# The second layers of a block's MLPs as seven products for eight, with sums made by adding DMAs

## The chip, the cores and the metric

The kernel runs on one core of a Trainium2 chip. The metric is the device time of one execution in microseconds (us); several executions are timed and their median is given. The core's engines each run an instruction stream of their own in program order: PE (TensorE, matrix products), DVE (VectorE), ACT (ScalarE), POOL (GpSimd) and SP (SyncE, which here only issues DMAs). The streams meet at semaphores. DMAs are issued from SP's queue and from POOL's queue. PE accumulates into banks of 128 x 512 numbers.

## The reference

One block of a model with gated cross-attention, on x of 2 x 512 tokens with 1024 numbers each, cut to what matters:

```python
x = x + tanh(g_xattn) * (fake_quant(layernorm(x)) @ fake_quant(ctx))
xt = layernorm(x).reshape(1024, 1024)
gate = ...                        # router: 16 experts in 4 groups, two experts a token
def step(y, p):
    w1, b1, w2, b2, w3, b3, ge = p
    h = silu(xt @ w1 + b1) * (xt @ w2 + b2)          # w1, w2: 1024 x 256
    return y + ge[:, None] * (h @ w3 + b3)           # w3: 256 x 1024
y = scan of step over the 16 experts
z = (silu(xt @ sw1 + sb1) * (xt @ sw2 + sb2)) @ sw3 + sb3      # sw1, sw2: 1024 x 512
x = x + tanh(g_ffn) * (y + z)
```

With these inputs the tokens use two experts in all. The hidden layer then has 512 numbers of the shared MLP and 256 of each expert, 1024 together, and the second layers are one product: h (1024 tokens x 1024) by w3 (1024 x 1024).

## The kernel before

The work has four stages. In the first (to about 100 us) x is normalised and quantised, multiplied with ctx, and the result added to x; x is stored to DRAM as `x_after`, 8 tiles of 128 tokens x 1024 (`xd`, L326). A second layernorm gives the operand of the MLPs. In the second stage the first layers of the shared MLP's first chunks of 128 hidden numbers and the router run.

From here on every product in fp32 is made of three: each operand is split into a high half, made by ACT (a cast, L333), and a low half, made by DVE (a difference, L334), and PE adds high·high, high·low and low·high.

The third stage makes the first layers of the hidden chunks 3 (`s3`) and 4 to 7 (`b4` to `b7`, the experts' chunks), each by a call of `pair` (L400). A pair takes w1's and w2's columns of one chunk and both batch rows as a 2 x 2 block product by Strassen's scheme: seven products of 12 matmuls of 512 columns (`product`, L405, matmul L410), in the order A11·B11, S2·T2, A12·B21, S3·T3, S1·T1, A22·T4, S4·B22, into three banks A, B and C in the order A B A B C B C. The sums S of the inputs are made once, by adding DMAs from POOL's queue (`add_x`, L786). The sums T of the weights are made by `prep_pair` (L378) for the next chunk while a pair runs: DVE makes four sums (L386 to L389) in two new slabs, then the splits. `prep_pair` is a generator: `begin` runs it to its first `yield`, each `go` on to the next, and the lists given to `pair` as `between` say after which product which steps are issued. Between the products a pair's own work on ACT, DVE and POOL makes the gated hidden numbers: ACT copies the first product (L430) and applies silu (L436, L447), DVE adds products (L433 s6, L440 and L443 s7, L446, L452 and the final multiplications L424), POOL multiplies by the router's gates (L421). `done` (L423) stores each half of a chunk to DRAM as `h_all`, from POOL's queue. The step of `between` that is issued after a product stands ahead of that product's own reading instruction on ACT and DVE.

Ahead of pair s3, SP issues the loads of b4's weights (`load_block`, L808, with the loads of L347: `e0a0r`, `e0b0r`) and stores the two experts' gate columns to DRAM as rows (`g_row`, L818), element by element, to be read back as `gates`, broadcast over partitions (L814). Then follow the next chunk's weights (`e0a1r`, `e0b1r`).

The fourth stage, the second layers, is `down_mm` (L871): 8 chunks x 8 tiles of 128 tokens x 2 halves of 512 columns x 3 = 384 matmuls of 512 columns (the last tile's second half in two of 256). `load_down` and `split_down` load the chunks of h and w3 again as 128 x 1024 and split them, the first six of them inside pair b7. Three token tiles are worked chunk by chunk, the others one after the other. `down_load` loads a tile of `x_after` into Y, `down_bias` (L912) adds the shared and the two experts' biases on DVE, scaled by tanh(g_ffn) and, for the experts, the token's gate (24 operations of 128 x 1024), and `down_end` (L916, L917) adds the scaled product and stores the result.

Tiles come from rings: `slab` (17 buffers of 128 x 1024), `octo` (14 of twice that), `temp` (7 of 128 x 512), `bank` (6) and `tbank` (2). A new tile waits until the last use of the buffer it is given has ended.

Of the kernel before, what the change touches and what calls it, by code (L numbers as in the profile page):

```python
# [9 lines left out]
F32 = mybir.dt.float32  # L10
# [8 lines left out]
P = 128  # L19
# [60 lines left out]
def flamingo_block(  # L80
# [19 lines left out]
    def slab(name, dtype, shape=(P, D)):  # L100
        return slabs.tile(list(shape), dtype, tag="slab", name=name)
# [20 lines left out]

    X = [None] * NT
    x_after = [spill.tile([P, D], F32, name=f"x_after{t}") for t in range(NT)]
    h_all = [spill.tile([P, B * S], F32, name=f"h_all{c}") for c in range(NC)]


    dq = [nc.sync]
# [170 lines left out]
    def fn(t, h):  # L299
        nm, r = md_[t]  # L300
        nc.vector.tensor_scalar(xn_[t][:, half(h)], X[t][:, half(h)], nm, r, ALU.add, ALU.mult)  # L301
# [30 lines left out]
    def split(raw, hi, lo):  # L332
        nc.scalar.copy(hi, raw)  # L333
        nc.vector.tensor_tensor(lo, raw, hi.bitcast(F32), ALU.subtract)  # L334
        return hi, lo

    def split_in_one(name, raw):

        both = octo(name, F32R, (P, 2, *raw.shape[1:]))
        return split(raw, both[:, 0], both[:, 1])  # L340
# [37 lines left out]
    def prep_pair(name, wa, wb, W):  # L378


        lo, hi = slice(0, KH), slice(KH, KD)
        two = lambda n: tuple(slab(f"{name}{n}{m}", F32R, (P, KD, P)) for m in "hl")
        ah, al = two("a")
        W["B11"], W["B21"] = (ah[:, lo], al[:, lo]), (ah[:, hi], al[:, hi])
        t13, t24 = slab(f"{name}t13", F32, (P, KD, P)), slab(f"{name}t24", F32, (P, KD, P))
        nc.vector.tensor_tensor(t13[:, lo], wa[:, lo], wb[:, lo], ALU.subtract)  # L386
        nc.vector.scalar_tensor_tensor(t24[:, lo], t13[:, lo], -1.0, wb[:, hi], ALU.mult, ALU.subtract)
        nc.vector.tensor_tensor(t13[:, hi], wb[:, hi], wb[:, lo], ALU.subtract)
        nc.vector.tensor_tensor(t24[:, hi], wa[:, hi], t24[:, lo], ALU.add)  # L389
        split(wa, ah, al)  # L390
        yield
        b22 = slab(f"{name}b22", F32R, (P, KD, P))
        W["B22"] = split(wb[:, hi], b22[:, lo], b22[:, hi])
        yield
        for n, t in (("24", t24), ("13", t13)):
            h, l = split(t, *two(f"t{n}"))
            W[f"T{n[0]}"], W[f"T{n[1]}"] = (h[:, lo], l[:, lo]), (h[:, hi], l[:, hi])
            yield

    def pair(name, W, b1, b2, ci, gates=None, between=()):  # L400


        pa, pb, pc = (bank(f"{name}{n}") for n in "ABC")
# [17 lines left out]
                nc.gpsimd.tensor_tensor(silu, silu, gates[:, ts(b, S)], ALU.mult)  # L421

        def done(h, silu, b):  # L423
            nc.vector.tensor_tensor(h, h, silu, ALU.mult)  # L424
            nc.gpsimd.dma_start(h_all[ci][:, ts(b, S)], h)

        s1, s6, s7, s11 = (temp(f"{name}{n}") for n in ("s1", "s6", "s7", "s11"))
        product(pa, "A11", "B11", True)
# [80 lines left out]
    def sup_post(c, b, got, lo=0, n=S):  # L509
        h = up_post(f"sa{c}_{b}_{lo}", got, sb1c(c), sb2c(c), n)  # L510
        nc.sync.dma_start(h_all[c][:, b * S + lo : b * S + lo + n], h)
# [245 lines left out]
    def go():  # L757
        next(prep[0], None)
# [2 lines left out]
    begin(3, raw3)  # L761
    go()
    go()
    sup_post(0, 1, got, 0, 256)
    go()
    lT = []
# [49 lines left out]
    load_block(SC)  # L816
    for j in range(2):
        nc.sync.dma_start(g_row[j].rearrange("(t p) -> p t", p=P), chosen[j][1])  # L818
    f = lambda fn, *a: (lambda: fn(*a))
    pair("s3", W[3], sb1c(3), sb2c(3), 3, None, (  # L820
        [f(split_x, "S1", s1)],
        [f(split_x, "S4", s4)],
        [f(lambda: begin(SC, raws_up[SC]))],
        [go],
        [go],
        [go, f(load_block, SC + 1), f(load_gates, 0)],
    ))
    down_prep = []
    for n in range(SC, NC):
        j, c = divmod(n - SC, EC)  # L830
        bv = chosen[j][2]
        if n + 1 < NC:
            between = (
                [f(begin, n + 1, raws_up[n + 1])], [], [go], [go], [go], [],
                [f(load_block, n + 2)] if n + 2 < NC else [],
            )
        else:
            between = down_prep
        if c == 0 and j == 1:
            load_gates(1)  # L840
        if n == NC - 1:
            break
        pair(f"b{n}", W[n], bv[:, 0, c : c + 1], bv[:, 1, c : c + 1], n, gates[j], between)


    def expert_row(w, e, c=None):
        if c is None:
            return w[ds(e, 1), :].rearrange("o d -> (o d)").partition_broadcast(P)
        return w[ds(e, 1), ts(c, P), :].rearrange("o p d -> (o p) d")

    def w3_rows(c):
        if c < SC:
            return sw3[ts(c, P), :]
        j, c = divmod(c - SC, EC)
        return expert_row(ew3, chosen[j][0], c)

    hid, w3, raw_down = [], [], {}

    def load_down(c):
        raw_down[c] = slab(f"h{c}r", F32), slab(f"d{c}r", F32)  # L860
        for raw, src in zip(raw_down[c], (h_all[c], w3_rows(c))):
            nc.sync.dma_start(raw, src)

    def split_down(c):
        for n, raw, got in zip("hd", raw_down[c], (hid, w3)):
            if c == 0:
                got.append(split(raw, *(slab(f"{n}{c}{m}", F32R) for m in "hl")))
            else:
                got.append(split_in_one(f"{n}{c}", raw))

    def down_mm(po, t, c, cols):  # L871
        (hh, hl), (wh, wl) = hid[c], w3[c]
        for p, cl in zip(po, cols):
            nc.tensor.matmul(p, hh[:, ts(t, P)], wh[:, cl], start=c == 0, stop=False)  # L874
            nc.tensor.matmul(p, hh[:, ts(t, P)], wl[:, cl], start=False, stop=False)  # L875
        for p, cl in zip(po, cols):
            nc.tensor.matmul(p, hl[:, ts(t, P)], wh[:, cl], start=False, stop=c == NC - 1)  # L877

    def bias_row(name, row):
        bb = slab(name, F32)  # L880
        dq[0].dma_start(bb, row)
        return bb

    n, bv = NC - 1, chosen[1][2]
    load_down(0)
    pair(f"b{n}", W[n], bv[:, 0, 1:2], bv[:, 1, 1:2], n, gates[1], (
        [f(load_down, 1)],
        [f(split_down, 0), f(load_down, 2)],
        [f(split_down, 1)],
        [f(split_down, 2), f(load_down, 3)],  # L890
        [f(split_down, 3), f(load_down, 4)],
        [f(split_down, 4), f(load_down, 5)],
        [f(load_down, 6)],
    ))

    gt = rt("gt", (P, 2, NT))
    for j in range(2):
        nc.vector.tensor_scalar(gt[:, j], chosen[j][1], tgf, None, ALU.mult)
    rows = []

    def load_rows():
        rows.append((bias_row("sb", sb3.partition_broadcast(P)), lambda t: tgf))
        for j in range(2):
            rows.append((bias_row(f"eb{j}", expert_row(eb3, chosen[j][0])), lambda t, j=j: gt[:, j, t : t + 1]))

    def down_load(t):
        X[t] = slab(f"Y{t}", F32)
        nc.sync.dma_start(X[t], x_after[t])

    def down_bias(t):  # L910
        for bb, scale in rows:
            nc.vector.scalar_tensor_tensor(X[t], bb, scale(t), X[t], ALU.mult, ALU.add)  # L912

    def down_end(po, t, cols):
        for p, cl in zip(po, cols):
            nc.vector.scalar_tensor_tensor(X[t][:, cl], p, tgf, X[t][:, cl], ALU.mult, ALU.add)  # L916
            nc.sync.dma_start(of[ts(t, P), cl], X[t][:, cl])  # L917

    halves = [half(0), half(1)]
    first, rest, last = (4, 5, 6), (7, 0, 1, 2), 3  # L920
    po = {t: [bank(f"po{t}_{h}") for h in range(2)] for t in first}
    for c in range(NC):
        if c == 0:
            split_down(5)
        if c == 1:
            load_down(7)
            split_down(6)
        if c == 2:
            split_down(7)
            load_rows()  # L930
            for t in first:
                down_load(t)
        if c == 4:
            for t in first:
                down_bias(t)
        for t in first:
            down_mm(po[t], t, c, halves)
    for t in first:
        down_end(po[t], t, halves)
    order = (*rest, last)  # L940
    for t in order[:2]:
        down_load(t)
    for n, t in enumerate(rest):
        down_bias(t)
        po = [bank(f"po{t}_{h}") for h in range(2)]
        for c in range(NC):
            down_mm(po, t, c, halves)
        down_end(po, t, halves)
        if n + 2 < len(order):
            down_load(order[n + 2])  # L950
    down_bias(last)
    for cl in (slice(0, 512), slice(512, 768), slice(768, 1024)):
        po = [bank(f"po{last}_{cl.start}")[:, : cl.stop - cl.start]]
        for c in range(NC):
            down_mm(po, last, c, [cl])
        down_end(po, last, [cl])
    manual.close()


# [47 lines left out]
                xl(t, h)  # L1007

    def mlp(name, n, up, down, b1, b2, row, scale):
        bb = bias_row(f"{name}bias", row)  # L1010
        for t in range(NT):
            nc.vector.scalar_tensor_tensor(X[t], bb, scale(t), X[t], ALU.mult, ALU.add)
        for c in range(n):
# [97 lines left out]
```

## Time and profile before

| | |
|---|---|
| median of 3 runs | 322.64 us (322.34 to 323.62) |
| profiled execution, its own time | 323.01 us |
| span of that execution in the trace | 321.3 us |
| granted PE clock, mean | 0.994 |
| busy: PE, DVE, ACT, POOL | 95%, 68%, 36%, 28% |
| pair s3, pairs b4 to b7 | 132.4 to 227.5 us |
| second layers on PE | 228.2 to 316.3 us |

The span is what the profiler recorded of one execution; its own time is 1.7 us longer and includes what lies around the span. "Busy" counts an engine's own instructions and not the waiting, nor the issuing of DMAs. A line of the chain of waits has a start, a duration and what it was; a line of a timeline has a start, a duration, the engine, the source line, the operation, and the tile written and those read, with shape and count. A name with "S", "l" or "h" at its end is a sum, a low or a high half. SPq is SP's queue of DMAs, q1 in the list of queues; q0 is POOL's.

### The profile page before, as it was taken

The numbers are of one execution on the slowest core, as the hardware profiler recorded it, in microseconds if no ns is written. First come the engines' busy times: TensorE is split into PE (matmuls) and PEld (weight loads), VectorE is DVE, ScalarE is ACT, GpSimd is POOL, SyncE is SP. The second block draws the span as 40 slices with busy tenths as digits, with TensorE's granted clock in tenths as the row PEclk, the third lists the DMA queues.
The fourth block names the chain that finished last, engine by engine and source line by source line (L and its number), as shares of the span: only waits on it lengthen the run. The fifth ranks groups of instructions, "written<-read, shape, count | busy, mean of one in ns | idle before, by whom it ended". The sixth has DMA issues, their size and how long they took to land.

```text
span 321.3 us, 4424 instructions
## 1 busy us (share of the span) xinstructions
PE 306.1 (95%) x1626; PEld 244.9 (76%) x1631; DVE 218.8 (68%) x360; ACT 116.2 (36%) x176; POOL 88.7 (28%) x130
## 2 busy tenths in 40 slices
PE   8588799999999999999999999999999999999993
PEld 2244695869995988888888888887788888888883
DVE  3869999997476886396657546479762975663261
ACT  2666669676545307361323324057610000000000
POOL 2695678896900322000013131112200000000000
PEclk9799999999999999999999999999999999999999
DMA  6999992029210999246341604459569053332121
GB/s 207 421 380 358 418 313 111 2 81 343 68 34 18 179 184 208 77 94 149 115 128 66 192 36 149 147 196 337 208 210 356 5 195 131 132 131 74 59 98 41
DMA packets 35105, 53.44 MB, mean 166 GB/s; under 512 B 5436, under 2 KB 23172, under 8 KB 35076
## 3 DMA queue, kind: packets, MB, share of 16 engines
q1 hardware_dynamic: 33124, 46.27, 42.0%
q0 software_dynamic: 1952, 6.82, 8.7%
q8 instruction: 15, 0.25, 0.3%
q14 instruction: 14, 0.11, 0.1%
HBM read 36.29 MB, written 12.59 MB: 152 GB/s over the span
## 4 chain that ended last, share of the span: by engine, by line
PE 83%; DVE 4%; DMA 4%; POOL 4%; issue 2%; ACT 2%; SPq 0%; DVEq 0%; POOLq 0%
PE sp L549 11%; PE sp L360 10%; PE po L877 9%; PE po L874 9%; PE po L875 9%; PE at L251 5%; PE b4B L410 3%; PE b6B L410 3%; PE b5B L410 3%; PE s3B L410 3%; DMA h4r<-h_all 2%; DMA X<-in_dram 2%; PE px L306 2%; PE b7A L410 2%; PE b5C L410 2%
## 5 line engine op out<-in xcount | busy, mean ns | idle before, releaser
L875 PE MATMUL po<-d,h 128*128 128x512 f32 (+1 forms) x119 | 44.9, 377 | 0.0
L874 PE MATMUL po<-d,h 128*128 128x512 f32 (+1 forms) x119 | 44.9, 377 | 0.0
L877 PE MATMUL po<-d,h 128*128 128x512 f32 (+1 forms) x119 | 36.9, 377 | 0.0
L251 PE MATMUL at<-cq,qT 128*128 128x512 bf16 x123 | 29.7, 379 | 2.9 <-POOL cq L170 1.7
L916 DVE SCALAR_TENSOR_TENSOR Y<-po,tg,Y 128x512 f32<-128x512 f32 (+1 forms) x17 | 11.4, 715 | 21.4 <-PE po L877 21.3
L875 PEld LDWEIGHTS po<-d,h 128*128 128x128 f32 x119 | 22.4, 188 | 4.1
L874 PEld LDWEIGHTS po<-d,h 128*128 128x128 f32 x119 | 22.4, 188 | 4.1
L877 PEld LDWEIGHTS po<-d,h 128*128 128x128 f32 x119 | 22.4, 188 | 4.1
L251 PEld LDWEIGHTS <-qT 128*128 128x128 bf16 x128 | 12.1, 97 | 15.7 <-issue 3.0
L912 DVE SCALAR_TENSOR_TENSOR Y<-eb,gt,Y 128x1024 f32<-128x1024 f32 x16 | 20.6, 1285 | 0.6
L912 DVE SCALAR_TENSOR_TENSOR Y<-sb,tg,Y 128x1024 f32<-128x1024 f32 x8 | 10.2, 1278 | 10.3 <-DMA Y<-x_after 10.3
L786 POOL DMA_DIRECT2D xf<-xf x8 | 7.2, 931 | 28.8 <-PE plt L649 15.0
L549 PE MATMUL sp<-XH,sb 128*128 128x256 f32 x96 | 14.1, 292 | 0.0
L549 PE MATMUL sp<-XH,sa 128*128 128x256 f32 x96 | 13.7, 288 | 0.0
L316 DVE TENSOR_TENSOR XL<-px,XH 128x512 fp32r<-128x512 f32 x16 | 10.4, 678 | 3.7 <-ACT xf L323 3.7
L549 PEld LDWEIGHTS sp<-XH,sb 128*128 128x128 f32 x96 | 12.3, 191 | 0.5 <-DVE sb L164 0.2
L360 PE MATMUL sp<-XH,sa 128*128 128x256 f32 (+1 forms) x64 | 12.5, 338 | 0.0
L360 PE MATMUL sp<-XH,sb 128*128 128x256 f32 (+1 forms) x64 | 12.5, 338 | 0.0
L549 PEld LDWEIGHTS sp<-XH,sa 128*128 128x128 f32 x96 | 12.3, 192 | 0.1
L272 ACT ACTIVATE xn<-X,s 128x512 f32<-128x512 f32 x16 | 11.4, 716 | 2.1 <-DVE X L263 1.8
L301 DVE TENSOR_SCALAR xn<-X,nm,d 128x512 f32<-128x512 f32 x16 | 11.2, 726 | 1.4 <-POOL d L297 1.3
L183 DVE BATCH_NORM_STATS2 st<-X 128x6 f32<-128x512 f32 x16 | 10.3, 680 | 2.3 <-DMA X<-in_dram 2.3
(499 smaller groups left out, 690.6 us busy)
## 6 DMA issues: line engine op xcount, KB each, us to landing
cr<-in_dram SPq DMA_DIRECT2D x15, 512.0 KB, 9.9
x_after<-X SPq DMA_DIRECT2D x8, 512.0 KB, 4.3
xf<-xf POOLq DMA_DIRECT2D x8, 512.0 KB, 5.1
Y<-x_after SPq DMA_DIRECT2D x8, 512.0 KB, 5.3
out_dram<-Y SPq DMA_DIRECT2D x15, 256.0 KB, 2.0
X<-in_dram SPq DMA_DIRECT2D x7, 512.0 KB, 9.0
h_all<-sa SPq DMA_DIRECT2D x8, 128.0 KB, 1.8
gates<-g_row SPq DMA_DIRECT2D x2, 512.0 KB, 5.3
```

Of the source, the lines that this page charges most:

```text
L251: nc.tensor.matmul(acc[t][h], qT[b][:, t % TB, k, :], cq[b][k // KH][:, k % KH, half(h)], start=(k == 0), stop=(k == KD - 1))
L272: nc.scalar.activation(xn_[t][:, half(h)], X[t][:, half(h)], AF.Square, bias=s[:, h : h + 1], scale=-float(H), accum_out=q[:, h : h + 1],)
L301: nc.vector.tensor_scalar(xn_[t][:, half(h)], X[t][:, half(h)], nm, r, ALU.add, ALU.mult)
L316: nc.vector.tensor_tensor(XL[b][q][p], px_[t, q], XH[b][q][p].bitcast(F32), ALU.subtract)
L360: nc.tensor.matmul(p, wx[:, k, :], xx[b][k // KH][:, k % KH, cols], start=first and k == 0, stop=last and k == KD - 1,)
L410: nc.tensor.matmul(p, w[:, k, :], x[:, k, :], start=f and k == 0, stop=l and k == KH - 1, skip_group_check=not first,)
L549: nc.tensor.matmul(up_[c, lo, i], w[:, k, :], x[0][k // KH][:, k % KH, lo : lo + 256], start=p == 0 and k == 0, stop=p == 2 and k == KD - 1,)
L874: nc.tensor.matmul(p, hh[:, ts(t, P)], wh[:, cl], start=c == 0, stop=False)
L875: nc.tensor.matmul(p, hh[:, ts(t, P)], wl[:, cl], start=False, stop=False)
L877: nc.tensor.matmul(p, hl[:, ts(t, P)], wh[:, cl], start=False, stop=c == NC - 1)
L912: nc.vector.scalar_tensor_tensor(X[t], bb, scale(t), X[t], ALU.mult, ALU.add)
L916: nc.vector.scalar_tensor_tensor(X[t][:, cl], p, tgf, X[t][:, cl], ALU.mult, ALU.add)
```

## The change

Second layers. The second product is made by Strassen's scheme over halves of the tokens (A1, A2), of the hidden numbers (shared, routed) and of the output columns. Seven products, each of 4 token tiles x 4 hidden chunks x 3 matmuls of 512 columns, 48 in all, make 336. Their order is A11·B11, A12·B21, S2·T2, nS3·nT3, A22·T4, S1·T1, S4·B22. The hidden numbers lie in two DRAM tensors (`h_dram`), shared and routed. The sums S of h are made by adding DMAs from DRAM onto a scaled copy or a loaded part (`add_part`), 8 of 512 KB; the sums T of w3 by DVE in place (`less`). The first product belongs to three further quarters of the output: `tell` scales it on ACT and adds it to `x_after` in DRAM by 12 adding DMAs of 256 KB. The other products' results are added to loaded parts of `x_after` by DVE, as before.

Biases. They are added to `x_after` in DRAM: the shared bias row is loaded broadcast (`load_shared_row`, behind the `g_row` stores on SP), multiplied by tanh(g_ffn) on ACT (`shared_row`), and added to the 8 tiles by adding DMAs of 512 KB from POOL's queue (`add_rows`) during pairs s3 and b4; the experts' rows are scaled by the tokens' gates and summed by ACT and DVE into small tiles (`sum_rows`, 16) and added by 16 DMAs of 256 KB (`add_sum`) during b4 to b7.

Weights' sums. `prep_pair` makes them in place, in the raw weights, in another order and with one more `yield`; it needs two slabs fewer. `done` stores h from SP's queue.

The diff, cut to its core:

```diff
-    h_all = [spill.tile([P, B * S], F32, name=f"h_all{c}") for c in range(NC)]
+    h_dram = [spill.tile([P, KH, B * S], F32, name=f"h{n}") for n in ("shared", "routed")]
+    h_all = [h_dram[c // SC][:, c % SC] for c in range(NC)]
...
     def prep_pair(name, wa, wb, W):
-        ah, al = two("a")
-        W["B11"], W["B21"] = (ah[:, lo], al[:, lo]), (ah[:, hi], al[:, hi])
-        t13, t24 = slab(f"{name}t13", F32, (P, KD, P)), slab(f"{name}t24", F32, (P, KD, P))
-        nc.vector.tensor_tensor(t13[:, lo], wa[:, lo], wb[:, lo], ALU.subtract)
-        nc.vector.scalar_tensor_tensor(t24[:, lo], t13[:, lo], -1.0, wb[:, hi], ALU.mult, ALU.subtract)
-        nc.vector.tensor_tensor(t13[:, hi], wb[:, hi], wb[:, lo], ALU.subtract)
-        nc.vector.tensor_tensor(t24[:, hi], wa[:, hi], t24[:, lo], ALU.add)
-        split(wa, ah, al)
+        h, l = split_in_two(f"{name}a", wa)
+        W["B11"], W["B21"] = (h[:, lo], l[:, lo]), (h[:, hi], l[:, hi])
+        nc.vector.tensor_tensor(wa[:, lo], wa[:, lo], wb[:, lo], ALU.subtract)
+        yield
+        nc.vector.tensor_tensor(wb[:, lo], wb[:, hi], wb[:, lo], ALU.subtract)
         yield
         b22 = slab(f"{name}b22", F32R, (P, KD, P))
         W["B22"] = split(wb[:, hi], b22[:, lo], b22[:, hi])
+        nc.vector.scalar_tensor_tensor(wb[:, hi], wa[:, lo], -1.0, wb[:, hi], ALU.mult, ALU.subtract)
+        nc.vector.tensor_tensor(wa[:, hi], wa[:, hi], wb[:, hi], ALU.add)
         yield
-        for n, t in (("24", t24), ("13", t13)):
-            h, l = split(t, *two(f"t{n}"))
+        for n, t in (("32", wb), ("14", wa)):
+            h, l = split_in_two(f"{name}t{n}", t)
...
         def done(h, silu, b):
-            nc.vector.tensor_tensor(h, h, silu, ALU.mult)
-            nc.gpsimd.dma_start(h_all[ci][:, ts(b, S)], h)
+            got = keep[0] if keep and b == 0 else h
+            nc.vector.tensor_tensor(got, h, silu, ALU.mult)
+            nc.sync.dma_start(h_all[ci][:, ts(b, S)], got)
...
+    def load_shared_row():
+        rows["s"] = slab("rows", F32)
+        nc.sync.dma_start(rows["s"], sb3.partition_broadcast(P))
+    def shared_row():
+        nc.scalar.mul(rows["s"], rows["s"], tgf)
+    def load_rows(h):
+        rows[h] = slab(f"row{h}", F32, (P, 2, H))
+        for j in range(2):
+            nc.sync.dma_start(rows[h][:, j], expert_row(eb3, chosen[j][0])[:, half(h)])
+    def sum_rows(h, t):
+        u = sums[h, t] = temp(f"u{h}_{t}")
+        nc.scalar.mul(u, rows[h][:, 0], gt[:, 0, t : t + 1])
+        nc.vector.scalar_tensor_tensor(u, rows[h][:, 1], gt[:, 1, t : t + 1], u, ALU.mult, ALU.add)
+    def add_rows(lo, hi):
+        for t in range(lo, hi):
+            nc.gpsimd.dma_start(x_after[t], rows["s"], accum_op=ALU.add)
+    def add_sum(h, t):
+        nc.gpsimd.dma_start(x_after[t][:, half(h)], sums[h, t], accum_op=ALU.add)
     pair("s3", W[3], sb1c(3), sb2c(3), 3, None, (
-        [f(split_x, "S1", s1)],
-        [f(split_x, "S4", s4)],
-        [f(lambda: begin(SC, raws_up[SC]))],
-        [go],
-        [go],
+        [f(split_x, "S1", s1), load_shared_row],
+        [f(split_x, "S4", s4), shared_row, f(add_rows, 0, 2)],
+        [f(lambda: begin(SC, raws_up[SC])), f(add_rows, 2, 4)],
+        [go, f(add_rows, 4, 6)],
+        [go, f(add_rows, 6, 7)],
         [go, f(load_block, SC + 1), f(load_gates, 0)],
+        [go, f(load_rows, 0)],
     ))
...
+    summed = [7 * n + k for n in range(3) for k in (1, 3, 4, 5, 6)] + [21]
+    for n, k in enumerate(summed):
+        steps[k].append(f(sum_rows, *divmod(n, NT)))
+        steps[k + 1].append(f(add_sum, *divmod(n, NT)))
+    steps[2].insert(0, f(add_rows, 7, 8))
...
+    def tell(t):
+        s = temp(f"u{t}")
+        nc.scalar.mul(s, pa[t], tgf)
+        for to, h in ((t, 1), (TB + t, 0), (TB + t, 1)):
+            nc.gpsimd.dma_start(x_after[to][:, half(h)], s, accum_op=ALU.add)
+    def product(p, a, b, first, post, meanwhile):
+        for t, steps in zip(range(TB), meanwhile):
+            down_mm(p[t], t, a, b, first)
+            post(t)
+            for step in steps:
+                step()
+    high("A12", parts=two)
+    low("A12", parts=two)
+    scaled("S2", "nS3", 1.0)
+    add_part("S2", h_part, 1, 1)
+    for t in range(TB):
+        down_load(t, 0)
+    pa = [bank(f"pa{t}") for t in range(TB)]
+    product(pa, "A11", "B11", True, tell, (
+        [f(low, "B21", parts=two), f(less, "T1", "B12", "B11", "B11")],
+        [f(less, "nT3", "B12", "B22", "B12")],
+        [f(less, "T2", "B22", "T1", "B22"), f(high, "T2", parts=one)],
+        [f(low, "T2", parts=one), f(high, "T2", parts=two), f(low, "T2", parts=two)],
+    ))
...
+    product(pa, "A12", "B21", False, lambda t: down_add(pa[t], t, 0, True), (
+        [f(high, "S2"), f(low, "S2", parts=one)],
+        [f(low, "S2", parts=two), f(scaled, "S4", "S2", -1.0), f(add_part, "S4", h_part, 1, 0)],
+        [f(high, "nS3"), f(low, "nS3", in_slabs, one)], [f(low, "nS3", in_slabs, two)],
+    ))
...
+    product(pb, "A22", "T4", False, lambda t: down_add(pb[t], TB + t, 0, True), (
+        [f(low, "S1", parts=two), f(high, "T1")], [f(low, "T1", parts=one)], [f(low, "T1", parts=two)],
+        [f(high, "S4"), f(low, "S4", parts=one)],
+    ))
+    pc = [bank(f"pc{t}") for t in range(TB)]
+    product(pc, "S1", "T1", True, lambda t: down_add(pc[t], TB + t, 1, True), (
+        [f(low, "S4", parts=two), f(high, "B22b")], [f(low, "B22b", parts=one)], [f(low, "B22b", parts=two)], [],
+    ))
...
```

The work of `load_down`, `split_down`, the old `down_mm`, `bias_row`, `down_bias` and `down_end` is removed. Pairs b4 to b6 get `begin` for the next weights after the first product and four `go` after the second to the fifth. Pair b7 gets the loads and splits of the first two products' operands between its products.

## The prediction

> **What bounds it now.** I read the table of stages first, then the chain of waits, then the timelines of DVE, ACT and the DMA queues around pair s3. In the table of stages (columns: busy time and instructions of each engine, granted clock, DMA share, GB/s) the pairs keep PE busy from end to end at clock 1.00, and DVE has room:
>
> ```profile
> 132.40:151.50 19.10, 19.10 (x86) 15.84 (x85) 15.27 (x18) 7.46 (x9) 0.22 (x1) 1.00 0.53 110
> 189.50:208.60 19.10, 19.10 (x86) 15.84 (x85) 11.55 (x15) 4.40 (x6) 3.71 (x5) 1.00 0.40 139
> 208.60:231.80 23.20, 22.86 (x100) 17.94 (x98) 18.24 (x20) 14.75 (x17) 4.81 (x6) 1.00 0.69 249
> 261.20:318.00 56.80, 55.06 (x266) 46.43 (x264) 28.59 (x30) 0.00 (x0) 0.00 (x0) 1.00 0.33 120
> ```
>
> So what is taken from PE here is gained, as long as nothing else becomes late. The chain gives PE's prices (start, duration, what): 2.72 us for a product of 12 matmuls of 512, or 0.227 us each, alike in both kinds of layer.
>
> ```profile
> 146.05 2.72 PE s3B L410 x12
> ...
> 208.61 2.72 PE b7A L410 x12
> ...
> 232.27 0.23 PE po L875
> ...
> 316.15 0.13 PE po L877
> 316.27 0.03 issue
> 316.30 0.48 DVE Y L916
> ```
>
> **Gain on PE.** From b7's start (208.61) to the last matmul's end (316.28) now: 107.67 us. After: 7 x 2.72 = 19.04 for b7, and 7 products x 48 = 336 matmuls x 0.2267 (2.72/12) = 76.17, together 95.21. Gain 12.5 us: 48 matmuls fewer are 10.9, and 1.6 are waits inside b7 and ahead of the last chunk, if the new stage has none. What follows the last matmul (DVE L916, a store, the end) stays: 5.1 us.
>
> **Cost of the shared bias row, first part.** The built program's order on SP is: the two weight loads of b4, both g_row stores (L818), then the new load of the sb3 row (512 KB, broadcast), then e0a1r. On ACT the new multiplication of that row stands ahead of the cast b4ah (L333), and on DVE b4al, which needs b4ah, and two sums stand ahead of s3s7 (L440), which reads bank s3B. PE's next product into that bank, A22·T4, waits for L440. Now that stretch runs so (start, duration, engine, line):
>
> ```profile
> 137.76 1.05 ACT L333 CAST b4ah<-e0a0r 128x1024 fp32r<-128x1024 f32 x1
> ...
> 142.24 1.22 DVE L334 TENSOR_TENSOR b4al<-e0a0r,b4ah 128x1024 fp32r<-128x1024 f32 x1
> ...
> 143.98 0.74 DVE L440 SCALAR_TENSOR_TENSOR s3s<-s3B,bT,s3s 128x512 f32<-128x512 f32 x1
> ```
>
> When does the row land? SP's timeline (start, duration of the issue), and the list of DMA issues between 130 and 160 (last column: us from issue to landing):
>
> ```profile
> 135.11 2.62 SPq L818 DMA_DIRECT2D g_row<-gv x2
> 140.64 0.38 SPq L347 DMA_DIRECT2D e0a1r<-in_dram  x1
> 143.49 0.38 SPq L347 DMA_DIRECT2D e0b1r<-in_dram  x1
> 148.40 1.76 SPq L814 DMA_DIRECT2D gates<-g_row  x1
> ```
>
> ```profile
> e0b0r<-in_dram SPq DMA_DIRECT2D x1, 512.0 KB, 4.7
> e0a1r<-in_dram SPq DMA_DIRECT2D x1, 512.0 KB, 11.4
> e0b1r<-in_dram SPq DMA_DIRECT2D x1, 512.0 KB, 10.1
> ...
> g_row<-gv SPq DMA_DIRECT2D x2, 4.0 KB, 13.0
> ```
>
> The g_row stores move 8 KB in all, in pieces of one number, and take 13.0 us; gates, which reads g_row, goes out at 148.40. The 512 KB queued behind them need 11.4 us, where e0b0r ahead of them needs 4.7. The row is issued right behind g_row, at 135.11 + 2.62 = 137.7. Lower bound: 3.8 us to land, the faster of the two gates loads (median 5.3, the one here 6.8), so 141.5. Upper bound: it lands with e0a1r, 140.64 + 11.4 = 152.0. I take 148.4 plus 512 KB at the 347 GB/s below, 1.5 us: L = 149.9, as e0a1r, its nearest neighbour, shows the wait. From L: ACT 1.05, cast 1.05, DVE 1.22 + 0.68 + 0.68 + 0.74, less the tenth by which neighbours overlap: 5.3. A22·T4, now at 146.05, starts at 149.9 + 5.3 = 155.2: **a stall of 9.2 us** (0.75 with L = 141.5, 11.2 with 152.0).
>
> **Cost of the shared bias row, second part.** The row's slab is used again by the high half of t14 of b5's weights, made in b4's fifth step. That cast waits for all eight adding DMAs (8 x 512 KB into x_after). The nearest row is the adding DMAs of L786; in the stretch 109 to 114 they ran alone:
>
> ```profile
> DMA packets 271, 1.00 MB, mean 199 GB/s; under 512 B 31, under 2 KB 31, under 8 KB 270
> ## 3 DMA queue, kind: packets, MB, share of 16 engines
> q0 software_dynamic: 270, 0.98, 99.7%
> ```
>
> Plain loads between 150 and 154:
>
> ```profile
> DMA packets 1664, 1.39 MB, mean 347 GB/s; under 512 B 46, under 2 KB 1508, under 8 KB 1664
> ```
>
> So an add of 524 KB keeps all 16 engines for 524/199 = 2.63 us, eight for 21.0. In the same time run the rest of e0a1r and e0b1r, gates, two stores of s3, half of the expert rows and the weight loads for b6, some 3.1 MB at 347 GB/s: 9 us. The first add starts 2.0 after L (ACT 1.05, POOL's issue 0.93), the last lands at L + 32.0. Behind it: cast 1.04, low half 1.22, a bias sum 0.69, L446 0.69, together 3.6, so L + 35.6. PE needs it for S4·B22 of b4, eight products after s3's A22·T4: L + 5.3 + 21.8 = L + 27.1. **Stall 8.5 us.** Bounds: the trace shows no add into DRAM. Nothing, if an add costs a plain copy's 1.5 us (12.1 + 9 + 2 + 3.6 = 26.7); 29.5, if the DRAM side doubles it (21 more). I take the measured add, the nearest row. An add holds its engines 1.7 times as long as plain bytes do (347/199).
>
> The Trainium skill ("Collectives: The Full Stack", on why ReduceScatter is half of AllGather) says an add needs two source reads and so runs at half a copy's rate, which speaks against putting 15 MB of adds into the span. By that rule an add would be 3.0 us, the eight 24.2, and the time some 3 us above my sum; the row says 2.63, and no row tells it for a target in DRAM.
>
> **What I cost at nothing.** DVE's bias sums and in-place sums: each pair gets five or six more operations of 0.7 us, 11.5 becomes about 15 of 19; without that room they would cost their 3.5 a pair. The expert sums' DMAs (16 x 1.3 us) hide in the pairs' DMA share of 0.35 to 0.4; small temporaries wait for them with some 3 us to spare. The h stores leave POOL for SP, where they wait for DVE L424 ahead of the half rows and the weight loads of the pair after next; a late half row delays b4's s6 by 1 to 3 us, inside the second stall. The new stage: each of 7 products takes PE 10.9 us, DVE has 4 x 0.74 of results and 3 to 6 us of preparation in it. The tightest operand by the program's order is T1's low half: its second part stands on DVE behind the third result of the fifth product, which PE ends 19.04 + 4 x 10.88 + 3 x 2.72 = 70.7 us after b7's start; with 0.74 and 1.22 it is ready at 72.7, and the sixth product begins at 73.4. So 0.7 us is the cover, and a result's DMA or an S later than its plain time eats it. The eight half-megabyte adds for S and the twelve quarter-megabyte ones of the first product need 21 + 16 us of the DMA engines, spread over 95.
>
> **Sum.** 321.3 - 12.5 + 9.2 + 8.5 = 326.5 of span, +5.2. The profiled execution took 323.01 and the median of the runs is 322.64, so I add the 5.2 to the median: 327.8, say **328**. About 1.6 us (0.5%) is what a measurement tells from no change.
>
> **Rivals.**
> Cheap adds (faster): the DMAs into DRAM run nearer to a copy than to L786's. Place: the cast of b5's t14. It decides from (27.1 - 2.0 - 9 - 3.6)/8 = 1.56 us an add downwards: 322.64 - 12.5 + 9.2 = 319.3; below 1.96 an add the whole change breaks even (a stall of 3.3). For it: L786's adds were issued two at a time, each waiting for an earlier one. Against: their engines were 99.7% taken.
> Early row (faster): the row's larger pieces pass g_row's in the queue, L = 141.5, and the second stall, which counts from L, stays: 322.64 - 12.5 + 0.75 + 8.5 = 319.4. For it: e0b1r, issued 2.9 us later than e0a1r, needed less. Against: both needed 10 us and more. With cheap adds too, 310.9, which is also the change with nothing late.
> Dear adds (slower still): the DRAM side doubles an add's time; it decides from 2.63 upwards; 327.8 + 21 = 349. For it: x_after and h must be read from DRAM besides the row. Against: nothing in the trace.
> It doesn't do what it says: the products of 512 keep their 0.227 us or not; the pairs, which already work in seven products, show that they do.
>
> **Numbers.** Forecast 0.57 (its own range 321 to 335, from L 146.5 to 152 and adds of 2.2 to 3.0), cheap adds 0.15, early row 0.10, both 0.05, dear adds 0.13. Faster: 0.30. Same: 0.07, the forecast's low end. Slower: 0.50 + 0.13 = 0.63. The range 311 to 335 takes in the faster cases and leaves out the dear adds and the edge of the double case.
>
> **What would show it.** The sb3 row's landing and the multiplication behind it at about 150; PE idle ahead of s3's A22·T4 for 9 us, released by DVE's s3s7; PE idle ahead of b4's S4·B22 for 8 us, with ACT's cast of b5's t14 waiting for an adding DMA; from b7 on 95 us to the last matmul, without a gap. The prediction is wrong if either gap is missing, or if the new stage waits for its S or T.

## The result, and the profile after

The changed kernel takes 358.98 us (median of 4 runs, 357.36 to 360.02), the kernel before 322.87: a ratio of 1.111 (95% interval 1.106 to 1.117), 36 us slower. The forecast had the side right and the size wrong: 328, with 335 as the end of the range. The profiled execution took 357.97, its span is 356.2, 34.9 more than the span before. All ratios here go by each kernel's fast runs; of the five runs of experiment 9, two took 334 us and are not in its ratio.

What PE waited for in the changed kernel (engine, tile and line; who ended the wait; us in total, times, longest):

```profile
PE s3B L412 <- DVE s3s L443: 11.0, 1, 11.0
PE pb L925 <- DVE Y L937: 9.5, 1, 9.5
PE b4B L412 <- DVE b4s L436: 6.6, 1, 6.6
...
PE pa L925 <- ACT u L990: 3.0, 1, 3.0
PE pb L925 <- DVE nT3l L908: 1.8, 1, 1.8
PE pb L925 <- DVE A22l L908: 1.6, 1, 1.6
```

With two short ones (0.6 and 0.4) these waits are 34.5 us. (L412 and L443 are L410 and L440 of the listing before; L925 is the new `down_mm`.) The stages of the changed kernel, columns as before:

```profile
132.40:150.00 17.60, 13.55 (x60) 10.89 (x58) 6.31 (x8) 2.48 (x3) 0.00 (x0) 0.99 0.81 107
150.00:170.00 20.00, 13.04 (x45) 10.51 (x46) 13.36 (x17) 7.42 (x9) 7.10 (x8) 0.67 1.06 236
170.00:190.00 20.00, 13.39 (x53) 10.59 (x52) 10.71 (x13) 5.67 (x8) 3.90 (x4) 0.83 0.79 183
...
190.00:210.00 20.00, 20.00 (x90) 16.57 (x89) 15.78 (x22) 8.42 (x12) 6.88 (x8) 1.00 0.84 176
...
290.00:310.00 20.00, 11.41 (x42) 8.75 (x41) 6.78 (x7) 5.99 (x6) 1.56 (x2) 0.83 1.11 250
310.00:330.00 20.00, 15.66 (x56) 12.32 (x57) 14.48 (x16) 5.78 (x6) 0.00 (x0) 0.75 0.46 175
```

Two things are to be seen. PE idles in pair s3, in b4 and in the second layers, not in b5 and b6. And in the stretches of 150 to 190 and 290 to 330 us, where it idled most, the granted clock (the column ahead of the DMA share) falls to 0.67 to 0.83. PE's timeline behind the first wait shows what that costs (start, duration; four matmuls take 1.07 at full clock):

```profile
156.96 2.08 PE L412 MATMUL s3B<-XH,b3t14h 128*128 128x512 f32 x4 [11.00 <-DVE s3s L443]
158.83 1.91 PE L412 MATMUL s3B<-XL,b3t14h 128*128 128x512 f32 x4
160.54 1.91 PE L412 MATMUL s3B<-XH,b3t14l 128*128 128x512 f32 x4
162.24 1.52 PE L412 MATMUL s3C<-S4h,b3b 128*128 128x512 f32 x4
163.60 1.07 PE L412 MATMUL s3C<-S4l,b3b 128*128 128x512 f32 x4
```

The account closes. From s3's first matmul (132.19) to the end of the last one (351.14) are 218.9 us. Five pairs at 19.04 and the new stage's 76.2 would be 171.4. The 47.6 between are 34.5 of waits and 13.1 of matmuls that took longer. Some 11 of these 13.1 are the clock: in the five stretches that the trace grants at 0.50, PE was busy for 22.1 us, half of it lost. The other 2 were not followed. Before, the same stretch had 1.6 to lose. So 47.6 - 1.6 - 10.9 (48 matmuls fewer) = 35.1, against 34.9 measured.

The chain of waits of the changed kernel tells what was late (start, duration, what). The first product of b7 and the last matmuls are in it too; they bound the stage for which the forecast had 95.2 us, and it took 351.14 - 231.37 = 119.8:

```profile
137.94 13.42 DMA rows<-in_dram
...
156.24 0.67 DVE s3s L443
...
166.40 12.38 DMA row<-in_dram
...
179.55 0.76 DVE b4s L436
...
231.37 2.72 PE b7A L412 x12
...
241.23 14.88 DMA rB<-in_dram
...
265.24 15.70 DMA x_after<-u
...
281.45 11.57 DMA x_after<-u
...
293.45 8.05 DMA out_dram<-Y
...
301.58 11.33 DMA Y<-x_after
...
349.44 1.70 PE pc L925 x12
```

The late ones are DMAs. The loads among them took two and a half to over three times the 4.7 us of a 512 KB load ahead of g_row: the shared bias row (landing at 151.36, forecast 149.9), half an expert's bias row (256 KB, for DVE's first bias sum, which stands ahead of b4's s6), and an operand of the second layers. Then come the first product's adds into x_after, for which SP's loads of Y wait: what stands behind these loads on SP, stores of the result and further loads of Y, goes out only at 293. SP's own waits between 228 and 330 (columns as for PE's):

```profile
SPq L933 <- DMA x_after<-u: 26.3, 4, 13.3
SPq L428 <- DVE b7s L427: 16.0, 1, 16.0
```

L933 loads Y, L428 stores h. The DMA engines were full, with adding DMAs above all. Between 153 and 177, and between 262 and 294 (lists of queues; q0 carries the adds):

```profile
DMA packets 1985, 5.51 MB, mean 230 GB/s; under 512 B 177, under 2 KB 512, under 8 KB 1985
## 3 DMA queue, kind: packets, MB, share of 16 engines
q0 software_dynamic: 1133, 4.17, 89.9%
```

```profile
DMA packets 4303, 8.04 MB, mean 251 GB/s; under 512 B 390, under 2 KB 390, under 8 KB 4300
## 3 DMA queue, kind: packets, MB, share of 16 engines
q0 software_dynamic: 2158, 4.00, 68.7%
```

### The profile page after: what moved, and what is told of

The parts are those of the page before. It is cut to its first block, busy times and chain, and to the rows that moved or that the text cites. A ratio compares the mean times of both kernels' runs of the same rounds, so it can differ in the third digit from the quotient of the medians.

```text
span 356.2 us, 4520 instructions
## 1 busy us (share of the span) xinstructions
PE 306.5 (86%) x1566; PEld 242.1 (68%) x1571; DVE 231.3 (65%) x380; ACT 146.9 (41%) x215; POOL 123.9 (35%) x164
## 4 chain that ended last, share of the span: by engine, by line
PE 54%; DMA 26%; issue 5%; DVE 5%; POOL 4%; ACT 3%; SPq 2%; DVEq 0%; POOLq 0%; ACTq 0%
PE sp L552 10%; PE sp L364 8%; DMA x_after<-u 8%; PE pc L925 6%; PE at L252 4%; DMA rB<-in_dram 4%; DMA rows<-in_dram 4%; PE pb L925 4%; DMA row<-in_dram 3%; DMA Y<-x_after 3%; PE b6B L412 2%; PE b5B L412 2%; DMA out_dram<-Y 2%; PE b4B L412 2%; DMA X<-in_dram 2%
## 5 line engine op out<-in xcount | busy, mean ns | idle before, releaser
L252 PE MATMUL at<-cq,qT 128*128 128x512 bf16 x123 | 30.7, 389 | 2.1 <-POOL cq L171 1.3
L857 POOL DMA_DIRECT2D x_after<-u x16 | 13.8, 865 | 44.2 <-DVE u L850 44.2
L937 DVE SCALAR_TENSOR_TENSOR Y<-pb,tg,Y 128x512 f32<-128x512 f32 x12 | 9.0, 749 | 22.9 <-DMA Y<-x_after 19.2
L850 DVE SCALAR_TENSOR_TENSOR u<-row,gt,u 128x512 f32<-128x512 f32 x16 | 13.0, 810 | 9.6 <-DMA row<-in_dram 8.8
L854 POOL DMA_DIRECT2D x_after<-rows x8 | 7.1, 2094 | 28.4 <-ACT rows L840 28.4
L849 ACT ACTIVATE u<-row,gt 128x512 f32<-128x512 f32 x16 | 11.4, 722 | 10.6 <-DMA row<-in_dram 7.2
L925 PE MATMUL pb<-T4h,A22h 128*128 128x512 f32 x16 | 7.4, 463 | 9.5 <-DVE Y L937 9.5
L992 POOL DMA_DIRECT2D x_after<-u x12 | 11.3, 1687 | 9.1 <-DMA rS<-hrouted 5.5
L937 DVE SCALAR_TENSOR_TENSOR Y<-pc,tg,Y 128x512 f32<-128x512 f32 (+1 forms) x9 | 6.2, 692 | 11.7 <-PE pc L925 11.7
L364 PE MATMUL sp<-XH,sa 128*128 128x256 f32 (+1 forms) x64 | 12.5, 338 | 0.0
L364 PE MATMUL sp<-XH,sb 128*128 128x256 f32 (+1 forms) x64 | 12.5, 337 | 0.0
L264 DVE SCALAR_TENSOR_TENSOR X<-at,cx_scale,X 128x512 f32<-128x512 f32 x16 | 11.6, 741 | 0.1
```

The source lines that it names most:

```text
L252: nc.tensor.matmul(acc[t][h], qT[b][:, t % TB, k, :], cq[b][k // KH][:, k % KH, half(h)], start=(k == 0), stop=(k == KD - 1))
L264: nc.vector.scalar_tensor_tensor(xs, acc[t][h], cx_scale, xs, ALU.mult, ALU.add, accum_out=sq_[t][0][:, h : h + 1])
L364: nc.tensor.matmul(p, wx[:, k, :], xx[b][k // KH][:, k % KH, cols], start=first and k == 0, stop=last and k == KD - 1,)
L849: nc.scalar.mul(u, rows[h][:, 0], gt[:, 0, t : t + 1])
L850: nc.vector.scalar_tensor_tensor(u, rows[h][:, 1], gt[:, 1, t : t + 1], u, ALU.mult, ALU.add)
L857: nc.gpsimd.dma_start(x_after[t][:, half(h)], sums[h, t], accum_op=ALU.add)
```

## Experiments

All ratios are to the kernel before, with their 95% intervals.

**1. The row ahead of g_row.** The call of `load_shared_row` goes away; the load stands behind `load_block(SC)`:

```diff
     load_block(SC)
+    rows["s"] = slab("rows", F32)
+    nc.sync.dma_start(rows["s"], sb3.partition_broadcast(P))
     for j in range(2):
         nc.sync.dma_start(g_row[j]...
```

> The load of the sb3 row is issued ahead of the two g_row stores on SP, nothing else. In the changed kernel PE waits 11.0 us for A22.T4 of pair s3 and runs some 2.6 us slower after it, at a lower granted clock. Theory (the row is late because it stands behind g_row): it lands by 143, the wait in s3 falls below 1 us, and the kernel takes 345 us (342 to 349); the later waits stay, and b4's wait for its half row may grow by 1 to 3. Rival (the row is late because the DMA engines are slow then, whatever the order): it lands at 148 or later, and the time moves by less than 4 us from 359.

354.56 us, 1.099 (1.096 to 1.103). The row landed at 143.1, 8.4 us after its issue; s3's wait fell from 11.0 to 3.2, not below 1 as I had expected, and behind it PE ran at half clock for 3.4 us instead of 6.2. These two make some 9 us. But only 4.4 us came out at the end (6.2 between the profiled executions): the wait behind the first product of the second layers grew from 3.0 to 5.0, and the one for nT3 from 1.8 to 3.5. The row's place is a cause; a third to a half of what it cost was waited for again further on.

**2. The row from POOL's queue.**

```diff
-        nc.sync.dma_start(rows["s"], sb3.partition_broadcast(P))
+        nc.gpsimd.dma_start(rows["s"], sb3.partition_broadcast(P))
```

> The load of the sb3 row is issued at the same place of the program, but from POOL's queue, so that no g_row store is ahead of it in its own queue. If only the order within SP's queue held it up, it lands by 143 and the time is that of the run with the row ahead of g_row, about 345 us. If g_row's small writes hold the engines themselves, it lands at 148 or later, the wait in s3 stays above 7 us, and the time is 354 to 360.

361.29 us, 1.120 (1.117 to 1.123). POOL came to the load at 127.8, ten us before SP, so the run doesn't tell whether SP's queue or the engines held the row up. It tells something else. s3's wait was gone, the adds began at 140.4, while the loads for the pairs were still under way, and the loads paid:

```profile
gates<-g_row SPq DMA_DIRECT2D x1, 512.0 KB, 26.0
row<-in_dram SPq DMA_DIRECT2D x2, 256.0 KB, 22.8
```

PE waited 19.2 us in b4, more than the 17.6 of both waits in the changed kernel.

**3. The row from ACT's queue**, in the second list of `between` of s3, behind S4's splits:

```diff
-        [f(split_x, "S4", s4), shared_row, f(add_rows, 0, 2)],
+        [f(split_x, "S4", s4), load_shared_row, shared_row, f(add_rows, 0, 2)],
...
+        nc.scalar.dma_start(rows["s"], sb3.partition_broadcast(P))
```

> The run with the row on POOL's queue issued it at 127.8, ten us before SP did, so it could not tell a slow queue from slow engines. Here the row is issued from ACT's own queue, behind the two casts of S4 (about 137.6; SP issues it at 137.9 in the changed kernel), while the g_row stores stand in SP's queue. If only SP's queue held the row up, it lands by 142, the wait in s3 falls below 1 us, and the time is near that of the run with the row ahead of g_row, 350 to 356. If g_row's small writes hold the DMA engines for every queue, it lands at 148 or later, the wait in s3 stays at 8 to 12 us, and the time is 357 to 361.

352.72 us, 1.092 (1.089 to 1.096). ACT's queue issued it at 134.67, ahead of the casts it was written behind and while SP issued g_row; it landed at 143.8, five us before g_row did, and s3's wait was 3.8. A row that is not queued behind g_row is early. Whether g_row's small writes would have held one issued after them on another queue stays open: no run had that order. Here the wait that I had forecast for b4 was seen: ACT's cast of b5's t14 waited 2.8 us for an adding DMA, and PE waited 0.3 us for b4's S4·B22 behind it (in run 1 the same, 2.7 and 0.2), where I had forecast 8.5.

**4. Without the eight adds of the shared row** (the shared bias is missing from the output):

```diff
         for t in range(lo, hi):
-            nc.gpsimd.dma_start(x_after[t], rows["s"], accum_op=ALU.add)
+            pass
```

> The eight adding DMAs of the shared bias row into x_after are left out (so the shared bias is missing from the output); the row is still loaded and multiplied. Theory (adds of 4 MB take the DMA engines from 153 to 175, so the experts' half row, issued at 165, lands at 178): the half row lands within 5 us, PE's 6.6 us wait for b4's S3.T3 and 2 us at the lower clock after it go, the wait in s3 stays at 11: 350 us (348 to 352). My prediction's mechanism (the cast of b5's t14 waits for the eight adds) would give the same time, but then the trace of the changed kernel should show that wait, and it does not. Rival (the half row is late because it is issued late): the wait stays above 4 us, 355 or more.

351.78 us, 1.092 (1.087 to 1.096). In the list of DMA issues and of PE's waits:

```profile
row<-in_dram SPq DMA_DIRECT2D x2, 256.0 KB, 4.7
```

```profile
PE s3B L412 <- DVE s3s L443: 11.1, 1, 11.1
PE pa L924 <- ACT u L989: 6.9, 1, 6.9
```

The half row takes 4.7 instead of 11.6, and b4's wait is gone: the adds made it. Again the second layers take something back: 6.9 instead of 3.0 behind the first product and 3.6 instead of 1.8 for nT3, while the wait for Y falls from 9.5 to 6.7.

**5. Without any adds into x_after**, the row ahead of g_row (both biases and the first product's share of three quarters of the output are missing):

```diff
     def add_sum(h, t):
-        nc.gpsimd.dma_start(x_after[t][:, half(h)], sums[h, t], accum_op=ALU.add)
+        pass
...
         nc.scalar.mul(s, pa[t], tgf)
-        for to, h in ((t, 1), (TB + t, 0), (TB + t, 1)):
-            nc.gpsimd.dma_start(x_after[to][:, half(h)], s, accum_op=ALU.add)
```

> The sb3 row ahead of g_row, and all adding DMAs into x_after left out: the shared row's eight, the experts' sums' sixteen and the first product's twelve (so both biases, and the first product's share in three quarters of the output, are missing). Their operands are still made. What is left is the second layer in seven products with its sums of h. Theory (what makes the kernel slow is the 11 MB of adds into x_after): no wait above 1 us from s3 to the end, span about 310, time 312 us (309 to 317). Rival (the seven products' own loads, sums of h and their order are late too): waits of 5 us or more remain behind b7, 320 us or more.

317.95 us, 0.985 (0.983 to 0.987). PE's waits from 128 on, and two stages that contain the first three products:

```profile
PE s3B L412 <- DVE s3s L443: 4.3, 1, 4.3
PE pc L921 <- DVE Y L933: 0.6, 1, 0.6
```

```profile
231.00:251.00 20.00, 20.00 (x90) 16.57 (x89) 16.39 (x17) 11.03 (x13) 3.71 (x3) 1.00 0.95 251
251.00:271.00 20.00, 20.00 (x90) 16.57 (x89) 14.44 (x16) 12.20 (x13) 4.88 (x4) 1.00 1.10 288
```

Behind s3 nothing waits longer than 0.6 us; s3's own wait I had not expected. The seven products, their sums of h and T, DVE's order and h's stores on SP hold as they are; the span, 315.6, is 321.3 - 12.5 = 308.8, 4.3 of s3's wait, 0.6 in the seventh product, some 1.4 of slow matmuls (2.8 us of busy PE at clock 0.50 behind s3's wait), and 0.5 not accounted for. Run 1 has the same place of the row and differs in the adds alone: 354.56 - 317.95 = 36.6 us are what the 11 MB of adds into x_after cost. The share of the DMA engines is 1.10 in the second stretch, as full as in the changed kernel though not for as long, and PE does not wait there: a full stretch alone does not stop it.

**6. The first product kept in SBUF**, added by POOL:

```diff
-            nc.gpsimd.dma_start(x_after[to][:, half(h)], s, accum_op=ALU.add)
+    def tell_on(to, h):
+        nc.gpsimd.tensor_tensor(X[to][:, half(h)], X[to][:, half(h)], told[to % TB], ALU.add)
```

> The changed kernel, but the first product A11.B11, scaled by ACT, stays in its four small tiles and POOL adds it to the loaded parts of x_after (12 operations of 128x512), instead of 12 adding DMAs of 256 KB into x_after in DRAM. Theory (in the second layers PE waits for loads of x_after that wait for these DMAs, and for operands that share the engines with them): the waits of 9.5 us (fourth and fifth product) and 1.8 us go, with some 2.5 us at the lower clock behind each; those ahead of b7's end stay: 343 us (340 to 348). Rival (the stage's other transfers fill the engines anyway): 352 or more. Rival (POOL's adds are late in their turn): DVE waits for POOL ahead of the third or fifth product.

344.08 us, 1.065 (1.057 to 1.074). PE's wait for Y:

```profile
PE pb L925 <- DVE Y L937: 0.9, 1, 0.9
```

The wait of 9.5 fell to 0.9, that for nT3 from 1.8 to 0.6; s3's (12.0), b4's (7.3) and the one behind the first product (3.4) stayed. The twelve adds cost some 15 us.

**7. h's stores back on POOL's queue.**

```diff
-            nc.sync.dma_start(h_all[ci][:, ts(b, S)], got)
+            nc.gpsimd.dma_start(h_all[ci][:, ts(b, S)], got)
```

> The changed kernel, but the stores of h are issued from POOL's queue, as before the change, not from SP's. In the changed kernel SP waits 10.7 us for DVE's last work of b6 with the loads for the second layers behind it, and PE then waits 3.0 us for ACT behind the first product. Theory A (that wait comes from SP's order): the loads go out 5 to 10 us earlier, the 3.0 us and 2.5 us at the lower clock go, and the half row in b4 goes out earlier: 350 us (347 to 354). Theory B (the DMA engines are full there whatever the order): within 2 us of 359.

344.86 us, 1.068 (1.064 to 1.072), 14 us less, where I had expected 9. PE's waits:

```profile
PE s3B L412 <- DVE s3s L443: 10.7, 1, 10.7
PE pb L925 <- DVE Y L937: 9.7, 2, 7.7
...
PE b4C L412 <- DVE b4s L446: 1.4, 1, 1.4
```

b4's 6.6 and the 3.0 behind the first product are gone, with their slow matmuls. On SP the loads stand behind stores that wait for DVE (16.0 and 10.7 us in the changed kernel), and so go out late. Run 5 had the same order and no wait: the order on SP costs only together with the adds into x_after. The 1.4 is a new wait in b4, where DVE waits 2.5 us for an adding DMA of an expert's sum.

**8. Both mended by POOL.** The shared row's halves are added by POOL into the experts' sums, and the first product as in run 6. All is computed; 4 MB of adds into x_after are left:

```diff
+        nc.gpsimd.tensor_tensor(sums[h, t], sums[h, t], srow[h], ALU.add)
         nc.gpsimd.dma_start(x_after[t][:, half(h)], sums[h, t], accum_op=ALU.add)
```

> Whole computation. The shared bias row is no longer added by eight DMAs of 512 KB: its halves are loaded beside the experts' half rows and added by POOL into the same 16 small sums, so that s3 has no row to wait for; and the first product is added by POOL to the loaded parts of x_after. The adds into x_after fall from 11 MB to the 4 MB of the 16 sums. Theory (the 7 MB that go were what made things late): no wait above 1 us from s3 on, span 309 to 311, time 312 us (310 to 316). Rival (the 4 MB still fill the engines when b7 fetches the second layers' operands): a wait of 3 to 7 us behind the first product, 318 to 323. Rival (POOL becomes the late one): DVE waits for POOL, 318 or more.

334.98 us, 1.037 (1.032 to 1.042). I had expected 312; both rivals came in. The wait behind the first product is 6.4 us, and DVE is late in pairs b4 to b6, by 1.0 to 1.8 a time, which I put down to POOL's added work; run 9 has these waits too, and no run took that work away alone. From DVE's and POOL's timelines:

```profile
272.00 5.50 DVE L902 TENSOR_TENSOR nS3l<-rnS,nS3h 128x1024 fp32r<-128x1024 f32 x1 [1.10 <-ACT nS3h L896]
...
278.08 1.21 DVE L902 TENSOR_TENSOR nS3l<-rnS,nS3h 128x1024 fp32r<-128x1024 f32 x1
```

```profile
270.74 5.66 POOL L989 TENSOR_TENSOR Y<-Y,u 128x512 f32<-128x512 f32 x4
```

DVE's 1.21 us operation takes 5.50 beside four of POOL's. They end at 276.40 and it ends 1.1 us later, about its own time: it ran only behind them. The Trainium skill ("SBUF — State Buffer", "SBUF: two separate sides") states a rule for this: the two engines share a pair of ports that one holds for a whole instruction, and the other is blocked. The row agrees, and here DVE got in between none of the four.

**9. The same with h's stores on POOL's queue.**

> As the run before, with the stores of h from POOL's queue. If nothing waits in that run, the same time within 1 us. If the loads behind SP's waits for DVE are what is late there, this one is faster by that wait; if POOL is the late one, slower.

327.80 us, 1.011 (1.005 to 1.017): some 7 us better than run 8. The one trace is of an execution of 334.26 us: the wait of 6.4 behind the first product is gone there, but 3.9 us for S2's low half and 3.1 in b7 have come. So it is not shown that the loads behind SP's waits made the difference.

**10. No adds into x_after, biases on PE.** The three biases of a token are a product over three rows (1 and the two gates, by the bias rows). With high and low halves side by side it is one matmul for each tile and half, into the bank that holds the result (two where a bank holds another quarter's too). DVE adds the first product in the fourth, sixth and seventh product.

```diff
+    def bias_mm(p, t, h, row="v", cl=slice(None)):
+        w = BIAS["n"] if row == "n" else BIAS["v"][:, half(h)]
+        nc.tensor.matmul(p, BIAS["g"][:, ts(t, P)], w[:, cl], start=False, stop=True, skip_group_check=True)
```

> Whole computation, no adding DMA into x_after. The three biases of a token (shared, two experts times gate) are a product over 3 rows, in high and low halves 9 rows of one operand, and PE adds them to a result's bank by one matmul of 512 columns (two where a bank already holds another quarter's), 20 in all, 20 x 0.227 = 4.5 us. The first product is added to the loaded parts of x_after by DVE (12 operations of 0.7 us) in the fourth, sixth and seventh product. Theory (the adds into x_after and the operations that made their operands were what made the change slow): as the run without any of these adds, 318 us, less its wait in s3 (4.3 and 2.6 at the lower clock), plus 4.5: 315.6 us (313 to 319), faster than before. Rival (DVE, full in the third and fourth product, is late with its four more operations): a wait of 1 to 3 us and 2.5 at the lower clock, 319 to 322.

320.0 us, 0.991 (0.989 to 0.994), where I had expected 315.6. One wait above 0.6 us is left, of my making: the splits of the bias operands stood ahead of b7's s7 on DVE.

```profile
223.71 2.08 PE L412 MATMUL b7B<-XH,b7t14h 128*128 128x512 f32 x4 [2.34 <-DVE b7s L443]
```

**11. The same with h's stores on POOL's queue.**

> As the run before, but the stores of h from POOL's queue. Without the adds into x_after nothing is late behind SP's waits for DVE: the same within 1 us. If the loads behind those waits are still late, faster by what PE waits behind b7 in that run.

321.35 us, 0.994 (0.992 to 0.997), the same wait, and 1.4 us more than run 10: without the adds into x_after, taking the stores off SP gains nothing.

**12. The splits two products later.**

```diff
-    last[2] += [f(low, "A11", in_slabs, two), f(high, "B11", parts=one), split_bias]
+    last[2] += [f(low, "A11", in_slabs, two), f(high, "B11", parts=one)]
+    last[4].append(f(split_bias, 0))
+    last[5].append(f(split_bias, 1))
```

> As the run with the biases on PE (stores of h from SP's queue), but the two casts and differences that split the bias operands stand behind the fifth and sixth product of b7 on ACT and DVE, not behind the third, where they waited for a buffer that PE was reading and held up DVE's s7, for which PE waited 2.3 us and then ran some 2 us slower. Theory: that wait goes and none takes its place: span 313 to 314, 315.6 us (314.5 to 317). Rival (the work only moves and DVE is late for the end of b7 or the second product): 318 to 320.

318.08 us, 0.983 (0.980 to 0.986): 1.7% faster than the kernel before, and faster than the changed one. Two waits of 0.7 and 0.6 are left in the second layers. It is 2.5 us above what I expected: in the profiled execution (319.57 us, the slowest of its runs) s3's first matmul starts at 133.8, 1.6 later than in the changed kernel. PE has a second stretch at half clock ahead of it, 3.4 us from 36.5 on; of the other traces only those of runs 2 and 6 have it, and their s3 starts at 133.6 and 133.8, in all others by 132.3. The rest I did not follow.

## Why the prediction was wrong

**The gain on PE, 12.5 us:** right. Run 5 shows it to within 0.5 us, once its two waits and the slow matmuls behind s3's are taken off.

**The first stall, 9.2 us:** the mechanism was right (row, ACT, b4al, s7, PE's A22·T4). The row landed 1.5 us later than forecast, and the wait was 11.0. The rival of the early row did not come about.

**The second stall, 8.5 us:** a wait came at b4, by the same adds, and 6.6 us long, but not by the path I gave. The half row, issued behind s3's store, ended it three products earlier, and the cast of t14 behind it had nothing left to wait for. Where the row came early, that path cost PE 0.2 and 0.3 us (runs 1 and 3). I had priced that half row at 1 to 3 us "inside the second stall". The size of the adds was right: their packets of 4096 bytes into DRAM took 328 ns in the trace, exactly as those into SBUF before (plain ones 159). So neither cheap nor dear adds. The rule of the Trainium skill that I had cited ("Collectives: The Full Stack", "The bandwidth ceiling: the fold count and why AG ≠ RS ≠ AR": an add at half a copy's rate) fits these packets to 3%.

**The clock:** a term that the sum did not have. Waits cost 34.5 us, and slower matmuls another 13.1, some 11 of them by half clock. Behind the forecast's own two stalls that alone was some 5 us.

**"What I cost at nothing":** this is the step that failed. From b7's start to the last matmul I had 95.2 us, "without a gap"; it took 119.8, of which 16.9 are waits and some 6 half clock behind them. Of the 29.7 us that the forecast span of 326.5 was short, 16.9 are these waits and 13.1 the slower matmuls of all stages; the two stalls missed by +1.8 and -1.9 and cancel, which is luck. I had added up the adds in that stage (21 + 16 us of the engines) and set them against 95 us; but the first product's 3 MB of adds, the sums of h and the loads of Y fall into the 50 us between 262 and 312, where the share of the DMA engines is 1.0 to 1.14 from 264 on. A full stretch alone did not stop PE in run 5; here the transfers are also in series: SP's loads of Y wait for the adds into the same rows, which POOL issues behind the adds of S2. Run 6, without these adds into x_after, took PE's wait for Y from 9.5 us to 0.9. I had written that a DMA later than its plain time eats the cover of 0.7 us, and had in the same document a price of 1.7 plain times for each add. The tightest operand was not T1's low half, as I had it: PE waited for Y (9.5 us), ACT's copy of the first product (3.0), nT3 (1.8) and A22 (1.6). The same holds for h's stores on SP: I had put them at the half row's 1 to 3 us, inside the second stall. They cost 14 us in the changed kernel (run 7), and nothing without the adds into x_after (runs 10 and 11).

The range failed with it: it held the bounds of the two stalls and none for the stage that I had taken as hidden. Its end of 335 was also added up wrongly: L = 152 and adds of 3.0 us make 333.

## What to carry to other kernels

A DMA that adds is cheap for the engines it relieves and dear for the DMA engines (328 ns a packet against 159 here): price it by packets in each stretch of the program, not against the span, and look at who waits for the same DRAM rows afterwards. A wait of PE costs its length and then, in most cases here, 1.6 to 3.1 us by matmuls at half clock. Taking one late transfer away partly moved the wait (run 1 gave back 3 to 5 of the 9 us that it took out of s3, run 4 1 to 2 of the 8 us of b4); only taking the adds into x_after away removed it. The adds for S, 4 MB, stayed in runs 5 and 10 to 12 and nothing waited long for them.

## What was not expected of the hardware

The clock does not follow each wait. After 11.0 us of idling it stayed at 0.50 for 6 us of work; a wait of 2.3 us (run 10) lowered it, one of 3.4 us (run 6) didn't. The stretches at 0.50 behind the waits last 3.41, 6.83, 10.24, 13.65 or 17.07 us, in every trace here a whole number of times 3.41. The Trainium skill ("TensorE: Matmul & The Clock Gate", "What's actually happening") has a free-running window of about 3.4 us behind this, which would make the outcome depend on where in the window the wait falls; these cases and lengths fit it, and no run here varied that alone.
